# Two matrix products of the second unit moved ahead of the first unit's third product, with their weights loaded between the halves of x

## The chip, the cores and the metric

The kernel runs on one core of a Trainium2 chip. The metric is device time in microseconds (us), the median of several executions. One more execution is recorded by the hardware profiler; all durations quoted here come from that one. Engines are called as in the profile: PE is TensorE, DVE is VectorE, ACT is ScalarE, POOL is GpSimd and SP is SyncE, whose queue issues most of the loads.

## The reference

Two layers with residuals are applied to x of shape (32, 128, 2048), in float32. The first is a linear layer with a bias and a low-rank adapter that is chosen for each sequence; the second is a linear layer whose whole weight matrix is chosen for each sequence.

```python
def reference(x, itok_B_1_7, itok_B_1_14, ...):
    # layer 0: base = x @ weight.T + bias;
    #          low = x @ a_sel.T; delta = low @ b_sel.T, adapter by itok_B_1_7
    x = x + (base + scale[:, None, None] * delta)
    # layer 1: w = weight[adapter_ids], adapter_ids = itok_B_1_14
    x = x + jnp.einsum('bij,bkj->bik', x, w)
    return x
```

## The kernel before, in words

**Two stages.** The first stage computes layer 0 for all sequences with one weight matrix, the second computes layer 1 for pairs of sequences with the weights of each. Both stages use the scheme of Strassen in Winograd's form: a block product of 2 x 2 blocks takes seven products in place of eight, and DVE makes sums and differences of the blocks before and after.

**The first stage in units.** `PHASES` lists seven phases, each a product of the outer level of the same scheme. A phase has two groups (two halves of the rows of x), a group has four units (four quarters of the output columns), so there are 56 units. Unit `n` has phase `i`, group `g` and column part `o`; `n // 4` is its group in the order of work. For one unit:

- Its weights are one tile W of 1 MB, 2 x 2 blocks. `w_sums(n)` makes four sums and differences of them on DVE: t1, t2 and t4 into the tile `tset` (two sets, by `n % 2`) and one in place. In the profile these are at line L181, of 128 x 512.
- Its x is that of the group: four quarters a11, a12, a21, a22 of 1 MB each, loaded as `add_a(group, 0)` to `add_a(group, 3)`. `a_sums(group)` makes s1 = a21 + a22, s2 = s1 - a11, a11 - a21 (in place of a21) and s4 = a12 - s2. For group 0, s1 and s2 are made in four pieces each, so that product 6 can begin with the first piece.
- `product(k, dst, n, start)` issues one of the seven products at line L486: four calls, each of 128 x 128 by 128 x 512, into one PSUM bank. The profile shows two records for each call, so eight for a product. The order in a unit is 1, 2, 6, 5, 7, 3, 4. Product 1 takes a11 and a block of W as loaded; product 2 takes a12 and another block of W as loaded. Product 6 takes s2 and t2, product 5 takes s1 and t1, product 7 takes a11 - a21, product 3 takes s4, product 4 takes a22 and t4.
- The banks are double: a unit with even `n` uses the first bank of each of `bank_a`, `bank_b` and `bank_c`, one with odd `n` the second. ACT copies products 1, 6, 5 and 7 out (`p1`, `u2`, `p5`, `u3`); DVE adds them up into the tile `z`. `finish(n - 1)` at the beginning of unit n stores or completes the unit before.

**Order of the work.** The schedule is manual: every engine does its instructions in the order in which the program writes them, and semaphores hold an instruction until its operands are there. Before the loop over the units, the weights' sums of unit 0 are made (`wts[0] = w_sums(0)`), then the sums of x of group 0. In the loop, `w_sums(n + 1)` is written at the beginning of unit n.

**Order of the loads.** The class `Loads` holds pools of slots in the tile `mem` and a list of loads; `pump` begins the loads in the order of the list as far as slots are free, and `done` frees a slot and pumps again. The first entries are made by `add_w` and `add_a`:

```python
        add_w(0)
        for q in range(4):
            add_a(0, q)
        add_w(1)
```

Unit 0's W and the quarter a11 come in halves: half of W, two halves of a11, the other half of W (lines L298 and L303); then a12, a21 and a22 (L320, 1 MB each) and W of unit 1 (L298, 1 MB). All these go through SP's queue. The list goes on with x of group 1 and W of later units.

**The second stage.** Each of 16 pairs of sequences has eight units of seven products (L682), with weights loaded at L211, sums of weights at L178 and L181 on DVE, and intermediate x loaded at L243.

Of the kernel before, what the change touches and what calls it, by code (L numbers as in the profile page):

```python
# [9 lines left out]
F32 = mybir.dt.float32  # L10
# [62 lines left out]
def cond_resid_kernel(  # L73
# [56 lines left out]
    nc = tc.nc  # L130
    B, S, D = out.shape
    NW, _, _, _, P, _, _, NF = w1q.shape
# [19 lines left out]
    units = [(i, g, o) for i in range(len(PHASES)) for g in range(2) for o in range(4)]  # L152
# [109 lines left out]
    with tc.tile_pool(name="c0", bufs=1) as c0, tc.tile_pool(  # L262
        name="ev", bufs=1
# [9 lines left out]
        bank_a, bank_b, bank_c = ([bank[:, 2 * k + m] for m in range(2)] for k in range(3))  # L273
# [13 lines left out]
        def add_w(n):  # L287
            i, g, o = units[n]
            for k, (_, r, c) in enumerate(PHASES[i][1]):
                halves = (0,) if n == 0 else (slice(None),)  # L290
                loads.add(
                    ("W", n, k), "W" if k == 0 else "st",
                    lambda slot, src=w0q[r, c, o], halves=halves: load_w(slot, src, halves),
                )

        def load_w(slot, src, halves):
            for h in halves:
                nc.sync.dma_start(out=view(slot, 2, 2, 4, P)[:, h], in_=src[:, h])  # L298
# [8 lines left out]
        def add_a(group, q):  # L307

            i, g = divmod(group, 2)
            t, h = divmod(q, 2)  # L310
            terms = [(r, k) for _, r, k in PHASES[i][0]]
            if i == LOW:
                terms += [(0, 1)]
                loads.add(("a", group, q), "st", lambda slot: load_a(slot, g, t, h))
            for m, (r, k) in enumerate(terms):
                loads.add(
                    ("A", group, q, m), "A" if m == 0 else "st",
                    (lambda slot, src=xq[r, g, t, k, h]: first_a(slot, src))
                    if group == q == 0
                    else lambda slot, src=xq[r, g, t, k, h]: nc.sync.dma_start(  # L320
                        out=view(slot, 4, NF), in_=src
                    ),
                )
# [29 lines left out]
                    )  # L353

        add_w(0)
        for q in range(4):
            add_a(0, q)
        add_w(1)
        for n in range(len(units)):
            if n // 4 + 1 < 2 * len(PHASES):  # L360
                add_a(n // 4 + 1, n % 4)
            if n + 2 < len(units):
                add_w(n + 2)
            add_end(n)
# [25 lines left out]
        def signed(sign, dst, src):  # L390
            (add if sign > 0 else sub)(dst, dst, src)
# [4 lines left out]
        def w_terms(n):  # L396

            for k, (sign, _, _) in enumerate(PHASES[units[n][0]][1]):
                if k:
                    signed(sign, mem[:, loads.slot(("W", n, 0))], mem[:, loads.slot(("W", n, k))])  # L400
                    loads.done(("W", n, k))

        def w_sums(n):

            w = w_view(n)
            t1, t2, t4 = (tset[:, n % 2, k] for k in range(3))
            sub(t1, w[:, 0, 1], w[:, 0, 0])
            sub(t2, w[:, 1, 1], t1)
            sub(w[:, 0, 1], w[:, 1, 1], w[:, 0, 1])
            sub(t4, w[:, 1, 0], t2)  # L410
            return {
                1: w[:, 0, 0], 2: w[:, 1, 0], 3: w[:, 1, 1], 4: t4, 5: t1, 6: t2, 7: w[:, 0, 1]
            }
# [11 lines left out]
        def a_sums(group):  # L425

            a11, a12, a21, a22 = (mem[:, loads.slot(("A", group, q, 0))] for q in range(4))
            s1, s2, s4 = (mem[:, k] for k in ((8, 9, 10), (9, 8, 10))[group % 2])
            acts[group] = {
                k: v.rearrange("p (i n) -> p i n", i=4)  # L430
                for k, v in {1: a11, 2: a12, 3: s4, 4: a22, 5: s1, 6: s2, 7: a21}.items()
            }
            if group == 0:
                for i in range(4):
                    some = ts(i, NF)
                    add(s1[:, some], a21[:, some], a22[:, some])
                    sub(s2[:, some], s1[:, some], a11[:, some])
            else:
                yield add(s1, a21, a22)
                yield sub(s2, s1, a11)  # L440
            yield sub(a21, a11, a21)
            yield sub(s4, a12, s2)
# [41 lines left out]
        def product(k, dst, n, start):  # L484
            for i in range(4):
                nc.tensor.matmul(  # L486
                    dst, lhsT=wts[n][k][:, i, :], rhs=acts[n // 4][k][:, i, :],
                    start=(start and i == 0), stop=(i == 3), skip_group_check=True,
                )
# [68 lines left out]
        acts, wts, b_sels = {}, {}, {}  # L558
        w_terms(0)
        wts[0] = w_sums(0)  # L560
        for _ in a_sums(0):
            pass
        w_terms(1)

        for n, (i, g, o) in enumerate(units):
            _, _, old, new, final = PHASES[i]
            a, b, c = (x[n % 2] for x in (bank_a, bank_b, bank_c))
            z = mem[:, 19 + n % 2]
            group = n // 4
            more = group + 1 < 2 * len(PHASES)  # L570
            lowering = more and (group + 1) // 2 == LOW
            apart = bool(new and final)
            late = final and not apart
            p1, u2, p5, u3 = (
                evp.tile([P, NF], F32, tag=k, name=k) for k in ("p1", "u2", "p5", "u3")
            )
            if n + 1 < len(units) and PHASES[units[n + 1][0]][4]:
                b_sels[n + 1] = load_b(n + 1)
            if n:
                finish(n - 1)  # L580
            if n == 2:
                make_scale()
            if n == len(units) - 2:
                load_w1(0)
            if n + 1 < len(units):
                wts[n + 1] = w_sums(n + 1)
            else:
                second_loads()
            sums = a_sums(group + 1) if more and o == 3 else iter(())

            product(1, a, n, True)
            nc.scalar.copy(p1, a)
            product(2, b, n, True)
            if lowering:
                lowrank(group + 1, o)
                loads.done(("a", group + 1, o))
            if more:
                a_terms(group + 1, o)
            if n + 2 < len(units):
                w_terms(n + 2)  # L600
            if lowering and o % 2 == 1:
                lowrank_out(group + 1, o // 2)
            if not late:
                add(zq(z, 0, 0), by_seq(b), by_seq(p1))
            product(6, a, n, False)
            nc.scalar.copy(u2, a)  # L606
            next(sums, None)
            product(5, c, n, True)
            nc.scalar.copy(p5, c)
            if n + 1 == len(units):  # L610
                second_sums(5)
            next(sums, None)
            if apart:
                add_low(n, [(0, bank_d, True), (1, bank_l, True)])
            product(7, a, n, False)
            nc.scalar.copy(u3, a)  # L616
            if apart:
                xs = view(loads.slot(("x", n)), 2, 2, NF)
                add(xs[:, 0, 0], bank_d, xs[:, 0, 0])
                add(xs[:, 0, 1], bank_l, xs[:, 0, 1])  # L620
            add(zq(z, 1, 1), by_seq(u3), by_seq(p5))
            next(sums, None)
            product(3, c, n, False)
            if apart:
                add_low(n, [(2, bank_d, True), (3, bank_l, True)])
            if not late:
                add(zq(z, 0, 1), by_seq(c), by_seq(u2))
            product(4, a, n, False)
            if apart:
                add(xs[:, 1, 0], bank_d, xs[:, 1, 0])  # L630
                add(xs[:, 1, 1], bank_l, xs[:, 1, 1])
            next(sums, None)
            if late:
                add_low(n, [(0, b, False), (1, c, False), (2, a, False), (3, bank_d, True)])
                add(zq(z, 0, 0), by_seq(b), by_seq(p1))
                add(zq(z, 0, 1), by_seq(c), by_seq(u2))
                add(zq(z, 1, 1), by_seq(bank_d), zq(z, 1, 1))
            nc.scalar.copy(zq(z, 1, 0), by_seq(a))  # L638
            loads.done(("W", n, 0))
            if o == 3:  # L640
                for q in range(4):
                    loads.done(("A", group, q, 0))
            if n + 1 == len(units):
                second_sums(4)
# [143 lines left out]
```

## Time and profile before

| | |
|---|---|
| median of 3 executions | 2994.54 us (2992.40 to 2995.85) |
| profiled execution, device time | 2994.32 us |
| profiled execution, span | 2992.7 us |
| mean granted PE clock | 0.999 |
| PE busy | 2976.9 us |
| DVE busy | 2337.7 us |
| ACT busy | 184.2 us |
| POOL busy | 239.8 us |
| first product starts | 6.84 us |
| PE without a gap from | 24.25 us |
| second stage's first matmul | 1443.12 us |
| moved by DMA | 1025.61 MB, mean 343 GB/s |

The span is the time from the first to the last recorded instruction of the profiled execution; its device time is 1.6 us more. Engines work beside each other, so busy times don't add up to the span. A matmul's end is modelled, and its record is a little longer than the time until the next one can start: two products in a row, 16 records, start 6.86 us before the one that follows them (28.65 to 35.51 us), while a product alone is shown with 3.60 us. Times on an engine's timeline are those from the span's start.

### The profile page before, as it was taken

The page shows a single profiled execution, that of the slowest core. Times are in us where ns is not written, and L with a number is a line of the kernel's source. Part 1 is how long each engine was busy: PE and PEld are TensorE (multiplying, and loading weights), DVE is VectorE, ACT ScalarE, POOL GpSimd, SP SyncE. Part 2 cuts the span into 40 slices and gives each one's busy share as a digit, 9 for nine tenths or more (in the row PEclk, how much of TensorE's full clock was granted, in tenths as well). Part 3 has the DMA queues.
Part 4 walks back from the last instruction along what each step waited for, and adds up shares of the span by engine and source line. Part 5 has one row for each costly group of instructions (what it writes and reads, how often), then busy time and mean ns, then how long its engine had stood idle before and what let it go on. Part 6 is the DMA issues. An engine that isn't in the chain of part 4 may idle for free.

```text
span 2992.7 us, 32904 instructions
## 1 busy us (share of the span) xinstructions
PE 2976.9 (99%) x12384; PEld 1178.5 (39%) x12384; DVE 2337.7 (78%) x1690; ACT 184.2 (6%) x313; POOL 239.8 (8%) x427
## 2 busy tenths in 40 slices
PE   9999999999999999999999999999999999999999
PEld 4445444444444444444333333333333333333333
DVE  3367755467655669773899999999999999999997
ACT  1111111111111111111000000000000000000000
POOL 1111000012222222221000000000000000000000
PEclk9999999999999999999999999999999999999999
DMA  5679966789866889985999999999999999999996
GB/s 225 239 307 360 343 255 253 266 316 353 311 246 225 305 341 392 393 311 207 367 394 390 390 387 404 388 395 390 402 390 394 393 385 404 385 398 385 407 387 226
DMA packets 186015, 1025.61 MB, mean 343 GB/s; under 512 B 23809, under 2 KB 23809, under 8 KB 79617
## 3 DMA queue, kind: packets, MB, share of 16 engines
q1 hardware_dynamic: 142432, 906.55, 76.5%
q0 software_dynamic: 25248, 83.92, 7.4%
q10 hardware_dynamic: 18176, 33.04, 3.5%
q8 instruction: 98, 1.61, 0.2%
q14 instruction: 61, 0.49, 0.0%
HBM read 922.76 MB, written 100.66 MB: 342 GB/s over the span
## 4 chain that ended last, share of the span: by engine, by line
PE 98%; DMA 1%; DVE 1%; SPq 0%; issue 0%; DVEq 0%
PE bank L682 51%; PE bank L486 44%; PE bank L497 1%; PE bank L453 1%; DMA mem<-in_w1q_dram 1%; DMA mem<-in_xq_dram 0%; DVE mem L181 0%; DVE mem L178 0%; SPq L211 0%; SPq L320 0%; SPq L303 0%; SPq L298 0%; DVE res L178 0%; SPq L243 0%; DVEq L178 0%
## 5 line engine op out<-in xcount | busy, mean ns | idle before, releaser
L181 DVE TENSOR_TENSOR mem<-mem 128x2048 f32<-128x2048 f32 (+1 forms) x733 | 1482.9, 2052 | 30.4 <-PE bank L486 6.3
L682 PE MATMUL bank<-mem 128*64 128x512 f32 x5120 | 1122.6, 593 | 4.4 <-DVE mem L181 2.4
L486 PE MATMUL bank<-mem 128*128 128x512 f32 x1792 | 792.5, 595 | 3.4 <-DMA mem<-in_xq_dram 3.4
L682 PEld LDWEIGHTS bank<-mem 128*64 128x64 f32 x5120 | 367.6, 137 | 737.0 <-issue 689.5
L486 PE MATMUL bank<-mem,tset 128*128 128x512 f32 x1344 | 597.6, 594 | 1.7 <-DVE mem L181 1.5
L486 PEld LDWEIGHTS bank<-mem 128*128 128x128 f32 x1792 | 338.3, 190 | 421.6 <-issue 417.1
L682 PE MATMUL bank<-mem,s 128*64 128x512 f32 x2048 | 461.2, 592 | 0.0
L178 DVE TENSOR_TENSOR mem<-mem 128x2048 f32<-128x2048 f32 (+2 forms) x193 | 338.7, 1769 | 124.9 <-ACT mem L638 56.9
L486 PEld LDWEIGHTS bank<-mem,tset 128*128 128x128 f32 x1344 | 253.7, 190 | 319.7 <-issue 315.7
L682 PEld LDWEIGHTS bank<-mem,s 128*64 128x64 f32 x2048 | 147.1, 137 | 292.4 <-issue 292.1
L178 DVE TENSOR_TENSOR mem<-u,p 128x512 f32<-128x512 f32 x56 | 38.7, 690 | 208.4 <-ACT u L616 208.4
L478 POOL DMA_DIRECT2D b_sel<-in_bt_dram x256 | 135.2, 528 | 580.7 <-PE bank L497 473.3
L178 DVE TENSOR_TENSOR mem<-bank,p 128x512 f32<-128x512 f32 x56 | 38.5, 687 | 126.1 <-PE bank L497 109.4
L688 ACT COPY pv<-bank 128x512 f32<-128x512 f32 x32 | 18.8, 586 | 1515.7 <-PE bank L682 1088.3
L178 DVE TENSOR_TENSOR pv<-bank,pv 128x512 f32<-128x512 f32 x64 | 44.3, 692 | 75.0 <-PE bank L682 74.0
L181 DVE TENSOR_TENSOR tset<-mem,tset 128x512 f32<-128x512 f32 x112 | 77.1, 689 | 8.9 <-PE bank L486 4.1
L178 DVE TENSOR_TENSOR mem<-mem,ident 128x1024 f32<-128x1024 f32 x64 | 78.0, 1219 | 0.0
L178 DVE TENSOR_TENSOR mem<-bank,u 128x512 f32<-128x512 f32 x56 | 38.4, 686 | 45.6 <-PE bank L486 45.6
L606 ACT COPY u<-bank 128x512 f32<-128x512 f32 x56 | 32.8, 586 | 391.8 <-PE bank L486 391.8
L638 ACT COPY mem<-bank 128x512 f32<-128x512 f32 x56 | 32.8, 586 | 387.0 <-PE bank L486 203.3
L533 POOL DMA_DIRECT2D x1t<-mem x64 | 49.2, 773 | 84.0 <-DVE mem L178 79.2
L497 PEld LDWEIGHTS bank<-low,b_sel 32*128 32x128 f32 x1024 | 39.1, 186 | 30.3 <-issue 27.3
(38 smaller groups left out, 519.2 us busy)
## 6 DMA issues: line engine op xcount, KB each, us to landing
mem<-in_w1q_dram SPq DMA_DIRECT2D x512, 1024.0 KB, 10.2
mem<-in_xq_dram SPq DMA_DIRECT2D x119, 1024.0 KB, 12.6
mem<-in_w0q_dram SPq DMA_DIRECT2D x111, 1024.0 KB, 6.9
mem<-U SPq DMA_DIRECT2D x40, 1024.0 KB, 9.0
mem<-in_xq_dram SPq DMA_DIRECT2D x66, 512.0 KB, 7.2
x1t<-mem POOLq DMA_DIRECT2D x64, 512.0 KB, 8.0
mem<-x1t SPq DMA_DIRECT2D x64, 512.0 KB, 9.1
out_dram<-res ACTq DMA_DIRECT2D x124, 256.0 KB, 6.0
```

The costliest lines, as they stand in the source:

```text
L178: nc.vector.tensor_tensor(dst, a, b, ALU.add)
L181: nc.vector.tensor_tensor(dst, a, b, ALU.subtract)
L453: nc.tensor.matmul(banks_r[r][ts(s, RT), :S], lhsT=a_sel[:, r, s, 4 * k + i, :], rhs=piece[:, i, s, :], start=(h == 0 and seen[r] == 0 and ...
L478: nc.gpsimd.dma_start(out=b_sel[ts(t, 2 * RT), s], in_=bt[ds(m, 1), c, o].rearrange("o j r m -> (o j r) m"),)
L486: nc.tensor.matmul(dst, lhsT=wts[n][k][:, i, :], rhs=acts[n // 4][k][:, i, :], start=(start and i == 0), stop=(i == 3), skip_group_check=True,
L497: nc.tensor.matmul(dst[:, ts(s, S)], lhsT=b_sels[n][ts(q, RT), s], rhs=low[r, g][ts(q, RT), s], start=start, stop=True, skip_group_check=True,
L533: nc.gpsimd.dma_start(out=x1t[4 * r + 2 * g + t][:, :, 8 * c + 2 * o : 8 * c + 2 * o + 2].rearrange("s p j m -> p s (j m)"), in_=view(19 + ...
L606: nc.scalar.copy(u2, a)
L638: nc.scalar.copy(zq(z, 1, 0), by_seq(a))
L682: nc.tensor.matmul(dst[ts(j, M)], lhsT=xts[pair, k4 // 2][k][:, j, k4 % 2 * 2 + i], rhs=w1s[n][k][:, j, i], start=(k4 == 0 and i == 0), st ...
L688: nc.scalar.copy(pv[:, 0], dst)
```

## The change

Three things are reordered, and nothing is added to the arithmetic:

1. On SP's queue, the load of unit 1's W comes after the quarter a12, ahead of a21 and a22.
2. On DVE, the four sums of unit 1's W are made right after those of unit 0's W, ahead of the sums of x. In the loop, unit 0 no longer makes them.
3. On PE, products 1 and 2 of unit 1 come right after products 1 and 2 of unit 0, ahead of unit 0's product 6. Unit 1 begins with its product 6. The copy of unit 1's product 1 out of PSUM goes to a tile of its own, `p1_next`, of 128 x 512 in the pool `c0`.

```diff
         add_w(0)
-        for q in range(4):
+        for q in range(2):
             add_a(0, q)
         add_w(1)
+        for q in range(2, 4):
+            add_a(0, q)
...
         wts[0] = w_sums(0)
+        w_terms(1)
+        wts[1] = w_sums(1)
         for _ in a_sums(0):
             pass
-        w_terms(1)
...
+            if n == 1:
+                p1 = p1_next
...
-            if n + 1 < len(units):
+            if 0 < n < len(units) - 1:
                 wts[n + 1] = w_sums(n + 1)
-            else:
+            elif n:
                 second_loads()
...
-            product(1, a, n, True)
-            nc.scalar.copy(p1, a)
-            product(2, b, n, True)
+            if n != 1:
+                product(1, a, n, True)
+                nc.scalar.copy(p1, a)
+                product(2, b, n, True)
+            if n == 0:
+                p1_next = c0.tile([P, NF], F32, tag="p1_next", name="p1_next")
+                product(1, bank_a[1], 1, True)
+                nc.scalar.copy(p1_next, bank_a[1])
+                product(2, bank_b[1], 1, True)
```

`w_terms(1)` does nothing in unit 1, since its phase has a single term of weights.

## The prediction

> **What bounds the kernel now.** I read the page first, then the list of waits for TensorE alone, then the chain of waits, and last the timelines of single engines over the first 30 us.
>
> ```profile
> span 2992.7 us, 32904 instructions
> PE 2976.9 (99%) x12384; PEld 1178.5 (39%) x12384; DVE 2337.7 (78%) x1690; ACT 184.2 (6%) x313; POOL 239.8 (8%) x427
> ```
>
> TensorE (PE) is recorded busy for all but 15.8 us of the span, at a granted clock of 0.999. The change adds and removes no matmul, so it can only win from those microseconds. All PE waits that have a releaser and lie in the first 45 us:
>
> ```profile
> PE bank L486 <- DMA mem<-in_xq_dram: 3.4, 1, 3.4
> PE bank L486 <- DVE mem L181: 1.5, 3, 1.1
> PE bank L369 <- POOL ident masks.py:199: 1.5, 1, 1.5
> ```
>
> The chain of waits (start, length, what) says what sets the start: the last quarter of x lands, VectorE (DVE) makes the sums s1 and s2 from it in four pieces, and from 24.25 us the PE runs without a gap.
>
> ```profile
> 4.16 14.54 DMA mem<-in_xq_dram
> ...
> 18.79 0.70 DVE mem L178
> ...
> 24.25 93.83 PE bank L486 x218
> ```
>
> PE's timeline (start, length, instruction, count) shows what it does until then:
>
> ```profile
> 6.84 3.60 PE L486 MATMUL bank<-mem 128*128 128x512 f32 x8
> 13.85 5.37 PE L486 MATMUL bank<-mem 128*128 128x512 f32 x8 [3.41 <-DMA mem<-in_xq_dram]
> 20.36 2.36 PE L486 MATMUL bank<-mem,tset 128*128 128x512 f32 x4 [1.13 <-DVE mem L181]
> 22.92 1.12 PE L486 MATMUL bank<-mem,tset 128*128 128x512 f32 x2 [0.20 <-DVE mem L181]
> 24.25 3.27 PE L486 MATMUL bank<-mem,tset 128*128 128x512 f32 x7 [0.20 <-DVE mem L181]
> ```
>
> A product is 4 calls, recorded as 8 matmuls. Sixteen of them run from 28.65 to 35.51, so one takes 0.429 us and a product 3.43 us. The first line is product 1 of unit 0, the second product 2, the rest is product 6 (third in order), fed piece by piece by DVE. Product 2 is slow: the stage table (window, length, busy time and count per engine, PEclk, DMA share, GB/s) gives
>
> ```profile
> 13.50:15.25 1.75, 1.40 (x4) 0.71 (x5) 0.00 (x0) 0.00 (x0) 0.00 (x0) 1.00 1.01 426
> 15.25:18.75 3.50, 3.50 (x6) 1.26 (x4) 0.00 (x0) 0.00 (x0) 0.00 (x0) 0.51 1.02 431
> 18.75:20.00 1.25, 0.47 (x2) 0.00 (x0) 1.18 (x2) 0.00 (x0) 0.00 (x0) 1.00 1.00 419
> ```
>
> Finer windows put the half clock between 15.26 and 18.68 us (0.76 in 15.0 to 15.5, 0.82 in 18.5 to 19.0): H = 3.42 us, which costs H/2 = 1.71 us. Today that is free, since product 6 waits for DVE anyway.
>
> **What the Trainium skill says.** "TensorE: Matmul & The Clock Gate", Part 1, states that a PE left idle falls to half its clock, that this is decided in free-running windows of 3413 ns, and that about one busy window brings the full clock back. The trace agrees: after 3.41 us without work, 3.42 us at 0.50. "DMA: Bandwidth & Descriptors", section "Queues, rings and completion order", states that each DMA engine takes a ring's descriptors in order. The trace agrees: the transfers of SP's queue land in the order of issue, 2.4 to 2.5 us apart. I use no price of either page.
>
> **The change, part by part.**
>
> *The load order.* SP's queue before (start, length of the issue):
>
> ```profile
> 2.28 0.43 SPq L298 DMA_DIRECT2D mem<-in_w0q_dram  x1
> 2.76 2.23 SPq L320 DMA_DIRECT2D mem<-in_xq_dram  x3
> 5.03 0.96 SPq L298 DMA_DIRECT2D mem<-in_w0q_dram  x1
> 6.03 0.44 SPq L320 DMA_DIRECT2D mem<-in_xq_dram  x1
> ```
>
> The x3 are the quarters a12, a21, a22; the line at 5.03 is W of unit 1. Issue plus time to landing gives 13.8 for a12 (2.76 + 11.0), 16.2 for a21 (3.62 + 12.6), 18.7 for a22 (4.16 + 14.5) and 21.1 for W1 (5.03 + 16.1). So 1 MB takes 2.45 us. The issues are out some 11 us before their landings, so their own 0.4 to 0.9 us cost nothing. With W1 moved past a21 and a22, a12 stays at 13.8, W1 lands at 16.2, a21 at 18.7, a22 at 21.15. Price: the data that s1 needs come **2.45 us later**. Behind them in SP's queue stand x of group 1, W2 and another piece of x, at the same places as before.
>
> *DVE's order.* Unit 1's four W sums go ahead of group 0's x sums. They took 28.52 to 31.13, 2.6 us. Now they start at about 16.3, when W1 is in, and end at 18.9. The x sums can't start before 21.2, so the moved work is hidden by DVE's wait for a22 (5.45 us long before); without that cover it would delay product 6 by up to 2.6. All x sums are late by 2.45: the four pieces of s2 release PE at 22.8, 24.1, 25.4 and 26.7 (before 20.36 to 24.25), the difference a11 - a21 is done at 28.9 instead of about 26.4, s4 at 31.05 instead of 28.6.
>
> *PE's order.* Two products, 16 matmuls, 6.86 us, move from unit 1 into the gap. PE from 13.85: product 2 of unit 0, products 1 and 2 of unit 1, product 6 of unit 0, 32 matmuls x 0.429 = 13.72, plus 1.71 for the half clock. Unit 1's product 1 can start at 13.85 + 3.43 + 1.71 = 19.0, and W1 is there since 16.2. Product 6 starts at 25.85 and its last piece at 28.4, after DVE's 26.7, so DVE no longer holds PE. Product 5 can start at **29.28**. Before, it started at 24.25 + 0.86 = 25.11, with the two products (6.86) still to do, so the same state came at 31.97. Gain **2.7 us**. In general it is 4.4 - H/2, where H is the time at half clock: with H = 0 PE would be through at 27.57, and DVE's last piece gives 27.58, so 4.4 is also the ceiling.
>
> *What else is late or loses cover.* Product 7 wants a11 - a21 at 29.28 + 3.43 = 32.7 (there at 28.9), product 3 wants s4 at 36.1 (31.05). W3's load waits for product 3 of unit 0 to be read: issued at 35.71 before, now at about 39.8. It took 4.8 us to land, and unit 3 starts only at about 84. The loads behind it on SP are for group 1, from about 84 on too. Unit 1 loses two products between unit 0's end (43.0) and its own product 6, which were cover for ScalarE's copy into u2: that copy comes at 46.4 and must wait for DVE's read of unit 0's u2, at about 40.3, 6 us earlier. DVE then makes W sums of unit 2 by 45.7, wanted at 67. POOL's store of unit 0's partial result goes from 40.03 to about 43.9, and nothing reads it for 150 us. ScalarE's extra buffer for product 1 of unit 1 (p1_next) replaces one copy of 0.59 us by another on an engine that is 6% busy: nothing.
>
> *Whether the lead lasts.* From 24.25 us on the chain is PE until the second stage begins. There PE waits three times:
>
> ```profile
> 1446.12 10.52 PE L682 MATMUL bank<-mem 128*64 128x512 f32 x48 [1.06 <-DVE mem L181]
> 1458.66 3.28 PE L682 MATMUL bank<-mem 128*64 128x512 f32 x8 [2.01 <-DVE mem L178]
> 1463.31 1.94 PE L682 MATMUL bank<-mem 128*64 128x512 f32 x8 [1.37 <-DVE mem L181]
> ```
>
> The loads behind these waits are issued at 1422 to 1424, after DVE's sums, after a PE product that ends at 1417.9. All of it hangs on PE's own progress and moves with it. After that PE runs without a gap, and SP's loads wait for PE or DVE. So I let all 2.7 us reach the end. The profiled execution took 2994.32 us, 0.22 under the median of the three runs shown (2994.54): 2994.32 - 2.7 = 2991.6, or 2991.8 from the median. I say **2991.7**. A measurement of this kernel tells about 0.2% (6 us) from no change; this gain is 0.09%.
>
> **Rivals.**
>
> 1. The half clock doesn't fall on this stretch (H = 0), because the windows lie otherwise against the kernel's start. For it: the windows are free-running by the page. Against: the gap ahead (10.44 to 13.85) is unchanged and as long as a window. It gives 4.4 us: 2989.9. Chance 0.2.
>
> 2. W1 doesn't really come ahead, because the transfers share the DMA engines and end together, at about 21.1. Then PE idles from 19.0 to 21.2, does unit 1's two products until 28.05 and product 6 until 31.5; the W sums push DVE's last piece to 29.3, still covered. The gain is 0.5 us: 2993.9. Against it: the even spacing of the landings. Likewise if the lead is lost at the second stage: 2994.3. Together 0.15.
>
> 3. **Slower**: the half clock stays on. All the added matmuls sit right behind the idle gap, so the time at half clock, free today, becomes a price of H/2. The sign turns at H = 2 x 4.4 = 8.8 us, two and a half times what the trace shows. If all 24 matmuls from 13.85 to product 6 ran at half clock (H = 20.6), product 6 would start at 34.4 and the change would lose 5.9 us: 3000.2. Against it: the full clock came back at 18.68 after 3.42 busy us, and the new order is busier. Chance of any loss 0.05.
>
> The forecast itself has 0.6.
>
> **How the numbers follow.** The three runs shown lie from 2992.40 to 2995.85, so a median moves by about 1 us unasked. The range runs from rival 1 less that scatter, 2988.8, to rival 2 and a small part of rival 3 plus scatter, 2995.4. Faster by over 0.2% would need more than 6 us, above the ceiling of 4.4, so scatter or a cause that I don't see: 0.05. Slower by over 0.2% needs H over 20.8 us or an unseen wait: 0.03. Within 0.2%: 0.92.
>
> **What would show it.** In the changed profile: W1 landing at about 16.2 and a22 at about 21.1; PE unbroken from 13.85, with 24 matmuls, then product 6; PEclk half for some 3.4 us after 15.3; no PE wait for DVE near 20 to 27; W sums of unit 1 ended before 19; the second stage's first matmul 2.7 us before 1443.12. Wrong would be a PE gap between 19 and 30, half clock for over 9 us, or a new wait at the second stage.

## The result, and the profile after

| | before | changed |
|---|---|---|
| median of 22 executions | 2994.05 us (2992.34 to 2996.49) | 2990.47 us (2987.76 to 2992.20) |
| ratio, 95% interval | | 0.9986 [0.998, 0.9992] |
| profiled execution, span | 2992.7 us | 2989.2 us |
| PE's unbroken run starts | 24.25 us | 13.25 us |
| second stage's first matmul | 1443.12 us | 1438.12 us |

The change makes the kernel 3.6 us faster, 0.14% with an interval from 0.08% to 0.2%. The forecast was 2991.7 us and "within 0.2%"; the size that it gave, 2.7 us, was a little low, and the measured time lies nearer to its first rival (2989.9 us, no half clock at the start).

"Half clock" stands below for a granted PE clock of 0.5, and H for the time that PE spends at it at the start. The page's head shows 2.5 us less PE time for the same matmuls, and a span 3.5 us shorter:

```profile
span 2989.2 us, 32900 instructions
PE 2974.4 (100%) x12384; PEld 1178.7 (39%) x12384; DVE 2337.5 (78%) x1690; ACT 183.9 (6%) x313; POOL 239.1 (8%) x427
```

The list of waits for PE over the whole span (who, for what: us in total, times, longest us) has lost the waits for DVE at the start: the three pieces of product 6 that waited no longer do.

```profile
PE bank L693 <- DVE mem L181: 3.6, 2, 2.7
PE bank L488 <- DMA mem<-in_xq_dram: 3.0, 1, 3.0
PE bank L693 <- DVE mem L178: 2.0, 1, 2.0
PE bank L371 <- POOL ident masks.py:199: 1.5, 1, 1.5
```

The chain of waits (start, length, what) now leaves DMA for PE 11 us earlier: it hangs on a12, issued at 2.76, and no longer on a22 and the sums of x.

```profile
2.76 10.36 DMA mem<-in_xq_dram
...
13.25 99.83 PE bank L488 x232
```

PE's timeline of the start:

```profile
6.70 3.60 PE L488 MATMUL bank<-mem 128*128 128x512 f32 x8
13.25 10.54 PE L488 MATMUL bank<-mem 128*128 128x512 f32 x24 [2.95 <-DMA mem<-in_xq_dram]
23.62 7.05 PE L488 MATMUL bank<-mem,tset 128*128 128x512 f32 x16
```

The 24 matmuls are the three products from product 2 of unit 0 on. They start 10.37 us before product 6, which is 24 x 0.432: full speed. The stage table (window, length, busy time and count for each engine, PEclk, DMA share, GB/s) agrees; where the kernel before showed a clock (PEclk) of 0.51, this execution shows 1.00:

```profile
15.25:18.75 3.50, 3.50 (x9) 1.52 (x8) 2.59 (x4) 0.00 (x0) 0.00 (x0) 1.00 1.04 438
```

On DVE the W sums of unit 1 come in the wait for a22, and the sums of x start at 20.66 (18.79 before):

```profile
15.63 0.69 DVE L181 TENSOR_TENSOR tset<-mem 128x512 f32<-128x512 f32 x1 [3.65 <-DMA mem<-in_w0q_dram]
...
17.57 0.68 DVE L181 TENSOR_TENSOR tset<-mem,tset 128x512 f32<-128x512 f32 x1
20.66 0.69 DVE L178 TENSOR_TENSOR mem<-mem 128x512 f32<-128x512 f32 x1 [2.40 <-DMA mem<-in_xq_dram]
...
25.37 5.09 DVE L181 TENSOR_TENSOR mem<-mem 128x512 f32<-128x512 f32 x3
```

The first of the last three is the last piece of s2. It ends at about 26.06, and PE wants it at 23.62 + 2.57 = 26.19: the two are level, which is where the forecast put its ceiling of 4.4 us.

The lead at the second stage's beginning is 5.00 us, and 3.5 us of it reach the end. PE's timeline there:

```profile
1438.12 1.94 PE L693 MATMUL bank<-mem 128*64 128x512 f32 x8
1440.95 10.52 PE L693 MATMUL bank<-mem 128*64 128x512 f32 x48 [0.90 <-DVE mem L181]
1453.49 1.94 PE L693 MATMUL bank<-mem 128*64 128x512 f32 x8 [2.01 <-DVE mem L178]
1458.14 7.07 PE L693 MATMUL bank<-mem 128*64 128x512 f32 x24 [2.71 <-DVE mem L181]
```

In the kernel before, the third of these groups took 3.28 us for its eight matmuls and was followed by a wait of 1.37; here the eight take 1.94 and the wait is 2.71. The sum is the same, 4.65 us, since DVE sets it: half clock over those eight cost nothing in that profile. The last wait ended at 1463.31 before and ends at 1458.14 now, a lead of 5.17. Now half clock falls behind that wait. The stage table:

```profile
1458.00:1460.00 2.00, 1.86 (x6) 0.58 (x8) 2.00 (x2) 0.00 (x0) 0.00 (x0) 0.70 0.96 387
1460.00:1462.00 2.00, 2.00 (x8) 0.62 (x6) 1.97 (x4) 0.00 (x0) 0.00 (x0) 0.50 0.32 127
1462.00:1464.00 2.00, 2.00 (x12) 0.67 (x10) 2.00 (x3) 0.00 (x0) 0.00 (x0) 0.95 0.93 236
```

2 x 0.30 + 2 x 0.50 + 2 x 0.05 = 1.70 us are lost, with PE busy all the time. 5.17 - 1.70 = 3.47 is the lead in the span.

So the theory that I took to the experiments was: the start follows the forecast's chain, with a gain of 4.4 - H/2 plus or minus what a12's landing scatters; whether H is 0 or 3.4 us differs from execution to execution; and half clock can cost time at the second stage too, where the forecast had put nothing. The rivals were that single parts of the edit bring the gain alone, and that DVE, not the clock, takes back the lead at the second stage.

### The profile page after: what moved, and what is told of

Its sections match the earlier page's. It is cut to its first block, busy times and chain, and to the rows that moved or that the text cites. A ratio compares the mean times of both kernels' runs of the same rounds, so it can differ in the third digit from the quotient of the medians.

```text
span 2989.2 us, 32900 instructions
## 1 busy us (share of the span) xinstructions
PE 2974.4 (100%) x12384; PEld 1178.7 (39%) x12384; DVE 2337.5 (78%) x1690; ACT 183.9 (6%) x313; POOL 239.1 (8%) x427
## 4 chain that ended last, share of the span: by engine, by line
PE 99%; DMA 1%; DVE 0%; issue 0%; SPq 0%; DVEq 0%
PE bank L693 51%; PE bank L488 45%; PE bank L499 1%; PE bank L455 1%; DMA mem<-in_w1q_dram 0%; DMA mem<-in_xq_dram 0%; DVE mem L181 0%; DVE mem L178 0%; SPq L303 0%; SPq L298 0%; DVE res L178 0%; DVEq L178 0%
## 6 DMA issues: line engine op xcount, KB each, us to landing
mem<-in_xq_dram SPq DMA_DIRECT2D x119, 1024.0 KB, 12.5
```

## The experiments

Each comparison has its own executions of the kernel before, on the same chip; their medians were 2995.69, 2995.29 and 2995.33 us in the three sets of four. Gains are differences of medians against these, intervals those of the ratio. A granted clock is the mean over a whole execution, rounded to three places: one stretch of 3.4 us at half clock takes 1.7 / 2990 = 0.0006 off and shows as 0.999, so 1.000 means no such stretch.

**Load order alone.** The kernel before with

```diff
-        for q in range(4):
+        for q in range(2):
             add_a(0, q)
         add_w(1)
+        for q in range(2, 4):
+            add_a(0, q)
```

> The kernel before with the load order of the change alone: W of unit 1 ahead of a21 and a22; no product and no W sum is moved. Theory (the start is a chain a22, sums of x, product 6, and a place in SP's queue is worth the transfer's own time): a22 lands 2.45 us later, PE's unbroken run starts at 26.7 us in place of 24.25, and the kernel is slower by 2.4 us than the one before. Rival (the transfers share the DMA engines and their order hardly matters): a22 still lands at about 18.7 and the time is that of before, within 0.5 us.

Measured: 2998.90 us, 3.2 us slower than before; ratio 1.0012 [1.0005, 1.0018]. The second stage begins at 1446.71, 3.59 us later. PE's timeline:

```profile
14.61 6.64 PE L488 MATMUL bank<-mem 128*128 128x512 f32 x8 [3.26 <-DMA mem<-in_xq_dram]
23.60 8.80 PE L488 MATMUL bank<-mem,tset 128*128 128x512 f32 x16 [2.34 <-DVE mem L181]
32.24 7.03 PE L488 MATMUL bank<-mem 128*128 128x512 f32 x16
```

The rival falls: a place in the queue ahead of x costs the chain. The surplus of 3.59 over 2.45 us has two parts in this profile. x landed later: product 2, which wants a12, starts at 14.61, not 13.85 (0.76 us). And products 6 and 5 ran partly at half clock: from the start of product 6 to that of product 7 it is 8.64 us here and 8.29 in the kernel before (0.35 us).

**Product and DVE order without the load order.** The changed kernel with the load order of before; the W sums of unit 1 stay moved too.

```diff
-        for q in range(2):
+        for q in range(4):
             add_a(0, q)
         add_w(1)
-        for q in range(2, 4):
-            add_a(0, q)
```

> The change without its load order: products 1 and 2 of unit 1 and its W sums go ahead, but W of unit 1 is still loaded behind a22. Theory: W1 lands at 21.1, PE waits for it from 17.3 or 19.0 on, does the two products until about 28.0 and product 6 until 31.5; gain 0.5 us against the kernel before, whatever the half clock does, since PE waits after it. Rival (moving the products is what pays, the place of the load is a detail): gain near that of the whole change, 3.6 us.

Measured: 2994.95 us, 0.7 us faster by the medians; ratio 1.0 [0.9991, 1.0008], so it is not clear of nothing, and the rival's 3.6 us (a ratio of 0.9988) lies outside. PE's timeline:

```profile
13.59 5.34 PE L486 MATMUL bank<-mem 128*128 128x512 f32 x8 [2.35 <-DMA mem<-in_xq_dram]
20.96 7.13 PE L486 MATMUL bank<-mem 128*128 128x512 f32 x16 [2.03 <-DMA mem<-in_w0q_dram]
27.93 7.03 PE L486 MATMUL bank<-mem,tset 128*128 128x512 f32 x16
```

The forecast's second rival had W1 at 21.1 and product 6 at 28.05; here they are at 20.96 and 27.93. The rival falls. The load order alone loses 3.2 us, the rest of the edit alone brings nothing that is clear of scatter, and together they bring about 4: the load order pays 2.45 us so that the products have something to do in that time.

**DVE order.** The changed kernel with the W sums of unit 1 behind the sums of x.

```diff
-        wts[1] = w_sums(1)
         for _ in a_sums(0):
             pass
+        wts[1] = w_sums(1)
```

> The whole change, but the W sums of unit 1 stay behind the sums of x of group 0 on DVE. Theory: the two moved products read W as loaded, so the W sums are not wanted before unit 1's product 6 at about 41 us; the place of these four instructions is worth nothing, and the time is that of the change (2990.5), within scatter. Rival (moving the W sums into DVE's wait is part of the gain): up to 2.6 us slower than the change.

Measured: 2992.99 us, 2.7 us faster than before; ratio 0.999 [0.9982, 0.9998]. That is 1.4 us less than the change brought in the next set, with intervals that overlap. The profile shows no wait for DVE at the start, but half clock there, as the forecast had it, and again behind the last wait of the second stage:

```profile
13.68 12.23 PE L488 MATMUL bank<-mem 128*128 128x512 f32 x24 [2.31 <-DMA mem<-in_xq_dram]
25.75 7.03 PE L488 MATMUL bank<-mem,tset 128*128 128x512 f32 x16
```

The second stage begins at 1440.23, a lead of 2.89. No execution of the 13 reached a clock of 1.000. So the place of the W sums costs nothing in the trace; whether the missing 1.4 us is half clock, which came in every one of these executions, or something that this profile doesn't show, these runs don't settle.

**Start kept busy.** The changed kernel with small matmuls in the wait for a12; `bank_l` is not used then.

```diff
                 product(1, a, n, True)
                 nc.scalar.copy(p1, a)
+                if n == 0:
+                    for k in range(9):
+                        nc.tensor.matmul(
+                            bank_l[:, :P], lhsT=ident, rhs=ident, start=True, stop=True)
                 product(2, b, n, True)
```

> The change with 9 small matmuls of the identity (about 3 us of PE) between product 1 and product 2 of unit 0, while PE waits for a12; their result is not used. Theory (the size of the gain is 4.4 - H/2, H the time at half clock after that wait, and H is 3.4 in some executions and 0 in others): PEclk stays 1.00 until 30 us in every look, and the time is that of the change or better by up to 1.7 us, by about 0.6 if a third of the executions fall to half clock. Rival (half clock never falls there in the changed kernel): no difference. If the small matmuls delay product 2, it is slower by that delay, under 0.3 us.

Measured: 2991.13 us, 4.6 us faster; ratio 0.9986 [0.9979, 0.9992]. In the profile the 18 records take 2.17 us, product 2 follows at once, and the start is at full clock. Half clock is left at the second stage, in this profile where DVE sets the pace (3.21 + 1.44 = 4.65 us again), so that it costs nothing there:

```profile
1453.58 3.21 PE L698 MATMUL bank<-mem 128*64 128x512 f32 x8 [2.01 <-DVE mem L178]
1458.23 12.24 PE L698 MATMUL bank<-mem 128*64 128x512 f32 x56 [1.44 <-DVE mem L181]
```

By executions, 5 of 21 have a clock of 1.000 (mean 2989.80 us) and 16 less (2991.36 us).

**The change again**, with nothing altered.

> The change itself once more, beside the three below, so that they share a chip. Theory: 3.6 us faster than the kernel before, within 1 us; in the profile either 1.7 us are lost at the start (half clock for about 3.4 us after 13 us, second stage beginning near 1440) or none (near 1438). Rival (the gain of the first comparison was partly chance): under 2.7 us.

Measured: 2991.17 us, 4.1 us faster; ratio 0.9988 [0.9981, 0.9994]. In this profile half clock came at neither place, with nearly the same waits: 2.41 us at the start (2.95 in the first profile), and at the second stage

```profile
1453.86 1.94 PE L693 MATMUL bank<-mem 128*64 128x512 f32 x8 [2.01 <-DVE mem L178]
1458.51 11.81 PE L693 MATMUL bank<-mem 128*64 128x512 f32 x54 [2.71 <-DVE mem L181]
```

54 matmuls take 11.81 us here, 0.22 each; in the first profile 24 took 7.07. Four of 21 executions have 1.000 (mean 2988.96 us), 17 have 0.999 (2991.49 us).

**The kernel before with its start kept busy.** The same nine calls ahead of product 2.

> The kernel before with the 9 small matmuls of the identity between product 1 and product 2 of unit 0. Theory (in the kernel before, the half clock at the start is free, because product 6 waits for DVE's sums anyway): PEclk is 1.00 over product 2, which takes 3.6 us in place of 5.4, PE then idles longer, and the time is that of before within 0.5 us. Rival (half clock costs the kernel before as well): faster by up to 1.7 us.

Measured: 2995.56 us against 2995.29; ratio 1.0002 [0.9994, 1.001]. Product 2 runs at full speed, and the time doesn't move:

```profile
13.36 3.60 PE L486 MATMUL bank<-mem 128*128 128x512 f32 x8
19.72 9.18 PE L486 MATMUL bank<-mem,tset 128*128 128x512 f32 x16 [2.76 <-DVE mem L181]
```

That fits the forecast's reading that product 2's half clock was free, but it is no clean test, for half clock then turns up behind the next wait, over product 6 (between 20.9 and 24.3, 1.7 us lost). From the start of product 6 to that of product 7, at 28.73, it is 9.01 us here and 8.29 in the kernel before: about 0.7 of the 1.7 us was not covered by DVE's pace. The direct evidence stays the trace of the kernel before, where PE waits 1.13 us for DVE right behind product 2. The second stage begins at 1443.21, as before.

**Both places kept busy.** The nine calls, and in the second stage

```diff
                 dst = bank[:, banks[k]]
+                for _ in range({(0, 7): 2, (1, 1): 5, (1, 7): 7}.get((n, k), 0)):
+                    nc.tensor.matmul(
+                        bank[:, 1, :P], lhsT=ident, rhs=ident, start=True, stop=True)
```

> The change with the 9 small matmuls at the start and 14 more at the second stage's beginning: 2 before product 7 of its unit 0, 5 before product 1 and 7 before product 7 of its unit 1, where PE waits for DVE. Their results are not used. Theory (what the profile of the change lost again after its lead of 5.0 us at the second stage's beginning is half clock there, 3.4 us long, now over matmuls that nothing else holds up): clock 1.000 in all executions, no half clock in the profile, and 0.5 to 1.7 us faster than with the start warmed alone, so 5 to 6 us faster than the kernel before. Rival (the lead is lost to DVE, which sets the pace there): PEclk 1.00 but no faster than with the start warmed alone.

Measured: 2989.39 us, 5.9 us faster; ratio 0.998 [0.9973, 0.9987]. All 18 executions have a clock of 1.000, and they lie within 1.4 us of each other (2988.44 to 2989.85; the change: 2988.43 to 2993.16). DVE's pace at the second stage is what it was: the starts below lie 12.5 and 4.65 us apart, as in the profile of the change (1440.95, 1453.49 and 1458.14). So the rival falls: it is the clock that took the lead back.

```profile
1441.49 10.52 PE L702 MATMUL bank<-mem 128*64 128x512 f32 x48 [0.45 <-DVE mem L181]
...
1454.02 1.94 PE L702 MATMUL bank<-mem 128*64 128x512 f32 x8 [0.70 <-DVE mem L178]
...
1458.67 11.81 PE L702 MATMUL bank<-mem 128*64 128x512 f32 x54 [0.96 <-DVE mem L181]
```

**The second place alone.** The 14 calls of the second stage, without those at the start.

> The change with only the 14 small matmuls at the second stage's beginning (2, 5 and 7 ahead of the three matmul groups that wait for DVE there); the start is that of the change. Theory (half clock at the second stage is a cost of its own, about 1.2 us on average, and adds up with that of the start): 5.1 us faster than the kernel before, between the change (3.9) and the change warmed at both places (5.7); executions at clock 1.000 near the latter. Rival (only the start matters; the second place is hidden by DVE): 3.9.

Measured: 2990.75 us, 4.6 us faster; ratio 0.9986 [0.9979, 0.9993], 0.5 below the 5.1 expected. Ten of 21 executions have 1.000 (mean 2989.46 us), 11 have 0.999 (2991.59 us). With both places kept busy every execution had 1.000, so what is left here is put down to the start: the wait for a12 led to half clock in about half of the executions, and these are 2.1 us slower in the mean (1.7 expected).

**The kernel before with both places kept busy.**

> The kernel before with the 9 small matmuls at the start and the 14 at the second stage. Theory (the second stage is the same in both kernels, so what half clock costs there is to be had without the change): 1.2 us faster than the kernel before, with half clock left at the start behind the new wait before product 6. Rival (the changed start shifted the second stage against the clock's windows, and the cost there belongs to the change): no faster than before.

Measured: 2994.46 us, 0.9 us faster; ratio 0.9997 [0.9989, 1.0005]. The interval takes in nothing and the 1.2 us alike: not settled. In this profile half clock at the start lay over products 6 and 5, for 6.8 us:

```profile
20.05 10.17 PE L486 MATMUL bank<-mem,tset 128*128 128x512 f32 x16 [2.82 <-DVE mem L181]
```

Product 7 starts at 30.05, 10.00 us after product 6 in place of 8.29, so 1.7 us are lost. In these two variants with a busy start, then, half clock was not free; the profile of the kernel before itself has none over product 6.

**Weights in halves.** More early work: the first half of W1 ahead of a12, and product 1 of units 1 and 2 early. In short:

```diff
-        for q in range(2):
-            add_a(0, q)
-        add_w(1)
-        for q in range(2, 4):
-            add_a(0, q)
+        # SP: W0 half, a11, W1 half, W0 half, a12, W1 half, W2 half, a21, a22, W2 half
...
+        # PE: P1(0), P1(1), P2(0), P2(1), P1(2), P6(0), P5(0), ...
```

> A further step: the weights of units 0, 1 and 2 are loaded in halves, in the order W0 first half, a11, W1 first half, W0 second half, a12, W1 second half, W2 first half, a21, a22, W2 second half; PE does product 1 of unit 0, product 1 of unit 1, product 2 of unit 0, product 2 of unit 1, product 1 of unit 2, then product 6 of unit 0. Theory (PE's start is worth what it does before a22's sums, and each half of W costs the chain 1.2 us): PE's wait for a12 is filled by product 1 of unit 1, product 2 of unit 0 starts 1.2 us later than in the change with 3.4 us more done, the half clock does not come since no wait is over 1.5 us, and DVE's last piece (about 28) stays ahead of PE: 2.2 us faster than the change, more where the change falls to half clock. Rival (the gap before a12 can't be filled, since the added half of W delays x by as much): within 0.5 us of the change.

Measured: 2989.34 us, 5.9 us faster; ratio 0.9981 [0.9975, 0.9988]. In this run unit 2's product 6 goes to another bank than its product 1, so the two are not added; the work is the same otherwise. The next run has unit 2 in the spare bank throughout:

```diff
             a, b, c = (x[n % 2] for x in (bank_a, bank_b, bank_c))
+            if n == 2:
+                a = bank_d
```

> The further step with weights in halves, with unit 2 using the spare bank for its products 1, 6, 7 and 4 throughout. Theory (the same work at the same places as in the run of that name before): 5.6 us faster than the kernel before, 1.7 faster than the change. Rival (the spare bank makes a new wait, at the low-rank products of group 1 that use it next, or the earlier gain was chance): under 4.5 us.

Measured: 2989.41 us, 5.9 us faster; ratio 0.9981 [0.9974, 0.9988]. No wait came with the spare bank. The waits of the start are 0.66 and 0.28 us:

```profile
11.97 3.70 PE L504 MATMUL bank<-mem 128*128 128x512 f32 x8 [0.66 <-DMA mem<-in_w0q_dram]
15.95 10.54 PE L504 MATMUL bank<-mem 128*128 128x512 f32 x24 [0.28 <-DMA mem<-in_xq_dram]
26.33 7.13 PE L504 MATMUL bank<-mem,tset 128*128 128x512 f32 x16
```

No half clock came at the start. At the second stage it came for twice the usual time, 2 x (2 x 0.47 + 2 x 0.50 + 2 x 0.50 + 2 x 0.23) = 6.8 us:

```profile
1454.00:1456.00 2.00, 1.24 (x4) 0.00 (x0) 1.97 (x2) 0.00 (x0) 0.00 (x0) 0.53 0.93 336
1456.00:1458.00 2.00, 0.54 (x2) 0.29 (x4) 2.00 (x2) 0.00 (x0) 0.00 (x0) 0.50 1.01 418
1458.00:1460.00 2.00, 2.00 (x6) 0.47 (x4) 2.00 (x2) 0.00 (x0) 0.00 (x0) 0.50 0.81 328
1460.00:1462.00 2.00, 2.00 (x10) 0.67 (x8) 1.97 (x4) 0.00 (x0) 0.00 (x0) 0.77 0.16 66
```

**The same, with the second stage kept busy.**

> The same with the 14 small matmuls at the second stage. Theory (both gains add up, and no wait over 1.5 us is left at the start): 6.8 to 7.4 us faster than the kernel before, the second stage's first matmul near 1437.8, clock 1.000 in every execution. Rival (one cause behind both): no faster than 5.9 us.

Measured: 2987.93 us, 7.4 us faster than before; ratio 0.9977 [0.9968, 0.9986]. All 11 executions have a clock of 1.000. This is the fastest version here, with nearly twice the gain of the change. Its second stage begins 6.5 us before that of the kernel before, and behind the last wait 56 matmuls run at 0.22 us each, so none of the lead is given back there:

```profile
1436.66 1.94 PE L724 MATMUL bank<-mem 128*64 128x512 f32 x8
...
1456.72 12.24 PE L724 MATMUL bank<-mem 128*64 128x512 f32 x56 [0.95 <-DVE mem L181]
```

## Why the prediction was right, and where its size was off

The step that carried the forecast was the sum for the start. It can be tested by the second stage's first matmul. With T the start of product 2 of unit 0 in a profile (13.85 in the kernel before) and 4.39 the forecast's 4.4 with one more digit, the sum says: 1443.12 - (4.39 - H/2) - (13.85 - T). It comes out within 0.03 us:

| profile of | T | H | by the sum | in the profile |
|---|---|---|---|---|
| the change | 13.25 | 0 | 1438.13 | 1438.12 |
| the change again | 13.29 | 0 | 1438.17 | 1438.15 |
| DVE order | 13.68 | 3.4 | 1440.26 | 1440.23 |
| start kept busy | 13.44 | 0 | 1438.32 | 1438.32 |
| both kept busy | 13.60 | 0 | 1438.48 | 1438.46 |
| second place kept busy | 13.21 | 0 | 1438.09 | 1438.08 |

- **The load order** was priced at 2.45 us for the chain. That DVE's sums of x started only 1.9 us later in the first profile of the change fits with a12's landing, 0.6 us earlier in the same execution. The experiment with the load order alone confirms the sign and, with what landed late, the size.
- **DVE's moved sums** were put into the wait for a22, and lie there. That their place is worth nothing is what the trace says.
- **Product 6 no longer waits for DVE**, at a margin of about 0.1 us, so the ceiling of 4.4 us was rightly placed. The lead beyond it, 5.00, is 4.4 plus the 0.6 us of a12's landing. That 0.6 is scatter between two executions and no gain of the change: T lies between 13.36 and 13.85 in the four profiles with the load order of before, and between 13.21 and 14.61 in those with the order of the change.
- **The loss of cover** in unit 1 and the later load of W3 made no wait on PE, and the lead lasts without a gap until the second stage.
- **The term H/2 was mis-sized.** The forecast took 1.71 us for every execution and gave H = 0 a chance of 0.2 as its first rival. In the executions where only the second stage was kept busy, 10 of 21 had no half clock at the start, so the term's mean is about half of what was put, some 0.9 us. The Trainium skill's page "TensorE: Matmul & The Clock Gate", Part 1, calls its windows free-running, and the forecast had cited that; the step that was off was to take the half clock of one profiled execution for the typical one. The runs agree with the page in this: half clock came and went between executions of one kernel.
- **The second stage was put at nothing**, since everything there hangs on PE's progress. The waits did move with PE. But the half clock behind them is not tied to PE's progress. The forecast showed a line with it, eight matmuls in 3.28 us, and did not price it: there it was free, in the first profile of the change it left its cover and cost 1.70 us, and with the start kept busy it was free again. In the means of all executions the start kept busy brought 4.5 us and both places 5.7, so on average half clock at the second stage costs the changed kernel some 1.2 us.
- **Whether that is a cost of the change is not settled.** The kernel before has the same waits there and may lose as much on average. Estimates from the figures above: if the 1.2 us fall on the changed kernel alone, the change should bring 4.4 - 0.9 - 1.2 = 2.3 us, and 4.4 with both places kept busy; 3.6, 4.1 and 5.9 were measured. If the kernel before loses the 1.2 us too, they should be 3.5 and 5.6, which fits much better, and the forecast's nothing would be right on average. Any other loss of some 1.2 us in the kernel before would fit as well. Its variant with both places kept busy gained 0.9 us with an interval that takes in nothing, so it stays open.
- **Some luck is in the total.** It came within 1.2 us although the half clock at the start was taken too large and that at the second stage was not looked into. The forecast's sign of half clock for 3.4 us after 15.3 did not show in the first profile of the change.
- **The third rival** (half clock staying on for 8.8 us or more) was not seen in any profile of the changed kernel. But stretches of 6.8 us came in four of the variants, twice what the forecast's trace showed; by the sum for the start, one there in the changed kernel would leave 4.4 - 3.4 = 1.0 us of the gain (an estimate).

## What to carry to other kernels

Work moved into a wait needs its data there: price the load that goes ahead of the others and the work that it makes possible as one sum, for alone each of the two may bring nothing or a loss. A state of the machine that hides under a wait, like half clock here, becomes a cost when the wait is filled; before counting on one profile for it, compare the granted clock of many executions. Where PE waits for a few microseconds just ahead of work that sets the end, small matmuls in the wait can save the half clock behind it (1.7 us for each 3.4 us here), though not the wait; look whether it comes back behind the next wait, as it did in the two variants of the kernel before.

## What the runs showed of the hardware

- Half clock came in stretches of 3.4 us (the kernel before at both places, the change at the second stage) or of 6.8 us (the load order alone and the kernel before with both places kept busy, at the start; both versions with weights in halves, at the second stage).
- It came after waits of 2.0 to 3.4 us, in about half of the executions at the start (11 of 21 with the second stage kept busy) and in 16 of 21 at the second stage (with the start kept busy). A wait's length alone did not decide it: at the start there was none after 2.95 us in the first profile of the change, and there was after 2.31 us in that of the DVE order.
- Nine calls of 128 x 128, 18 records in 2.17 us, were enough to hold the full clock even with 0.66 us of wait left over, and 7 calls with 0.95 us left.
- In SP's queue a place ahead cost the transfers behind it the whole time of the transfer: 2.45 us for 1 MB by the landings in the kernel before, and 3.2 us of kernel time in the run with the load order alone, where other parts came to it.
